# A convolution kernel whose half sums m1 and m2 move into two PSUM tiles of one bank each

## The chip, the cores and the metric

One core of one Trainium2 chip. The metric is the device time of one execution in microseconds. Medians are over four to eleven executions. A ratio is the mean time of one kernel's runs over the mean of the other's of the same rounds, so it is not quite the ratio of the medians quoted beside it.

## The reference, cut to what matters

```python
w   = (v1 + v2).reshape(OUT_CH * N, IN_CH, 3, 3)      # U quantised in two steps
act = conv_general_dilated(gn(x), w, padding=1, feature_group_count=5)
return x + act        # x: (160, 128, 32, 32) fp32, gn: group norm without affine
```

That is 160 images of 128 channels and 32 x 32 pixels, in five sets of 32 that each have their own 128 x 128 x 3 x 3 weights. Each image is normalised, convolved and added to itself.

## The kernel before

The vertical direction of the 3 x 3 filter is computed on pairs of rows. TensorE makes two half sums per image, m1 and m2 (16 x 32 fp32 for each of 128 channels, one PSUM bank each). The even rows of the output start from m1 + m2 and the odd rows from m1 - m2. TensorE then adds the rest of the convolution on top, in a two-bank PSUM tile `eo`, of which there are two. PSUM is the memory into which TensorE writes its sums; a half sum fills one bank of it. To evacuate a tile is to read it out of PSUM, so that TensorE can write it again; the residual is the addition of the convolution to x. Images come in two kinds. A "combined" image has both of its 16-bit parts combined beforehand, so m2 takes six matmuls and m1 six. A "direct" image has three and three, and a longer rest.

```python
self.pair = self.ps_m.tile([P, 2, self.H // 2, self.W], F32, tag="m", name="m")   # two banks, one tile

def sums_of_pairs(self, i):                    # TensorE: m2 first, then m1
    for a, kind in ((1, self.DIFF), (0, self.SUM)):
        for col in self.COLS: ...              # 3 or 6 matmuls into m[:, a]

def leave(self, i):                            # ScalarE: m2 to SBUF
    self.nc.scalar.copy(m2, self.pair[:, 1])

def pairs(self, i, between=lambda: None):      # VectorE: m1 from PSUM, m2 from SBUF
    m1, m2 = self.pair[:, 0], self.m2.pop(i)
    nc.vector.tensor_add(rows[:, :, 0], m1, m2)
    between()                                  # one other small instruction
    nc.vector.tensor_sub(rows[:, :, 1], m1, m2)
```

A steady iteration i, by engine, in the order of the program, in which the traces show them as well:

```
TensorE: m2(i+1), m1(i+1), rest of the convolution of i
ScalarE: statistics, sum(i-1) out of PSUM, copy of m2(i+1), high part of i+3, statistics
VectorE: low part of i+2 (direct: its combinings), add and sub for i+1, combine(i+4)
POOL:    accumulating DMA of sum(i-1) onto x in SBUF;   SyncE: store, then load ahead
```

Tracking of reads and writes goes by tile. In the built program TensorE signals once, after the last matmul of m1. ScalarE's copy of m2 waits for that signal, and the next m2 waits for VectorE's subtraction, which of this tile reads m1 only.

## Time and profile before

| | before |
|---|---|
| time, median (range) | 1043.2 us (1041.9 to 1045.2) |
| TensorE / VectorE / ScalarE busy | 953.6 / 931.0 / 897.1 us of 1038.9 |
| waits around m: VectorE / ScalarE / TensorE | 84.5 / 83.2 / 48.8 us |
| ScalarE waiting for loads of images | 11.1 us, three times |

The lines behind the busy times and the waits around m are shown in the prediction. The shares of the chain of work that ended last, of which the three engines hold 83%:

```profile
ACT junk L192 <- DMA xt<-in_x_dram: 11.1, 3, 10.2
```

```profile
PE 42%; DVE 29%; ACT 12%; issue 7%; POOL 5%; DMA 5%; SPq 0%; POOLq 0%; ACTq 0%; DVEq 0%
```

Of the page's part on DMA (packets, MB, share of the time of 16 engines), these two:

```profile
q1 hardware_dynamic: 45168, 173.09, 49.1%
q0 software_dynamic: 22032, 80.23, 39.9%
```

The first queue carries loads and stores. The second carries the accumulating transfers within SBUF, which add the convolution to x.

### The profile page before, as it was taken

The numbers are of one execution on the slowest core, as the hardware profiler recorded it, in microseconds if no ns is written. First come the engines' busy times: TensorE is split into PE (matmuls) and PEld (weight loads), VectorE is DVE, ScalarE is ACT, GpSimd is POOL, SyncE is SP. The second block draws the span as 40 slices with busy tenths as digits, with TensorE's granted clock in tenths as the row PEclk, the third lists the DMA queues.
The fourth block names the chain that finished last, engine by engine and source line by source line (L and its number), as shares of the span: only waits on it lengthen the run. The fifth ranks groups of instructions, "written<-read, shape, count | busy, mean of one in ns | idle before, by whom it ended". The sixth has DMA issues, their size and how long they took to land.

```text
span 1038.9 us, 16017 instructions
## 1 busy us (share of the span) xinstructions
PE 953.6 (92%) x5935; PEld 573.6 (55%) x5935; DVE 931.0 (90%) x1253; ACT 897.1 (86%) x1215; POOL 433.7 (42%) x599
## 2 busy tenths in 40 slices
PE   2899998999999999999999999999899999999996
PEld 1445555555555555555555555565555555565554
DVE  7999999998989999889999998899999988888884
ACT  4779898989889898998998989888998999998561
POOL 4546653452515172634443544417262623243320
PEclk9999999999999999999999999999999999999999
DMA  9439899989999989999999999998999999997664
GB/s 367 174 102 246 241 245 264 234 234 272 291 250 256 266 233 258 251 273 263 245 261 256 251 258 257 283 260 236 258 264 244 240 269 273 272 258 210 172 162 145
DMA packets 67287, 254.42 MB, mean 245 GB/s; under 512 B 5248, under 2 KB 5248, under 8 KB 67200
## 3 DMA queue, kind: packets, MB, share of 16 engines
q1 hardware_dynamic: 45168, 173.09, 49.1%
q0 software_dynamic: 22032, 80.23, 39.9%
q8 instruction: 48, 0.79, 0.3%
q14 instruction: 39, 0.32, 0.1%
HBM read 89.19 MB, written 83.89 MB: 167 GB/s over the span
## 4 chain that ended last, share of the span: by engine, by line
PE 42%; DVE 29%; ACT 12%; issue 7%; POOL 5%; DMA 5%; SPq 0%; POOLq 0%; ACTq 0%; DVEq 0%
PE m L670 18%; PE eo L634 15%; PE eo L670 7%; DVE eo L738 4%; DVE vl L587 4%; DVE eo L740 4%; ACT vh L581 4%; DVE v L570 3%; ACT junk L199 3%; DMA xt<-in_x_dram 3%; DVE v L573 2%; DVE v L576 2%; DMA xt<-sum 2%; ACT m L728 2%; DVE lo L594 2%
## 5 line engine op out<-in xcount | busy, mean ns | idle before, releaser
L670 PEld LDWEIGHTS <-wt 128*128 128x128 f16 x4428 | 428.9, 98 | 295.9 <-DVE eo L740 62.2
L767 POOL DMA_DIRECT2D xt<-sum x153 | 138.1, 903 | 434.5 <-ACT sum L754 424.6
L634 PE MATMUL eo<-hi,wt 128*128 128x496 f16 (+3 forms) x1260 | 300.9, 375 | 1.1 <-ACT wt L479 0.6
L670 PE MATMUL m<-vh,wt 128*128 128x512 f16 x534 | 203.4, 381 | 48.2 <-DVE eo L740 48.0
L587 DVE SCALAR_TENSOR_TENSOR vl<-v,rstd,vh 128x2048 f16<-128x2048 f32 x89 | 208.7, 2345 | 1.2 <-ACT vh L581 1.1
L670 PE MATMUL eo<-vl,wt 128*128 128x248 f16 (+1 forms) x1068 | 204.7, 273 | 0.0
L670 PE MATMUL eo<-vh,wt 128*128 128x248 f16 (+1 forms) x1068 | 204.6, 273 | 0.0
L670 PE MATMUL m<-vl,wt 128*128 128x512 f16 x534 | 202.9, 380 | 0.0
L634 PEld LDWEIGHTS <-wt 128*128 128x128 f16 x1332 | 130.0, 99 | 127.9 <-ACT wt L479 1.8
L738 DVE TENSOR_TENSOR eo<-m,m 128x512 f32<-128x512 f32 x157 | 109.1, 695 | 84.6 <-ACT m L728 84.5
L581 ACT ACTIVATE vh<-v,rstd 128x2048 f16<-128x2048 f32 x89 | 178.6, 2007 | 4.6 <-POOL v L560 3.7
L199 ACT ACTIVATE junk<-xt,mv 128x1024 f16<-128x1024 f32 x152 | 173.7, 1143 | 0.2
L192 ACT ACTIVATE junk<-xt 128x1024 f16<-128x1024 f32 x152 | 160.7, 1057 | 14.2 <-DMA xt<-in_x_dram 11.1
L754 ACT ACTIVATE sum<-eo 128x1024 f32<-128x1024 f32 x153 | 154.6, 1010 | 14.2 <-PE eo L670 13.3
L728 ACT COPY m<-m 128x512 f32<-128x512 f32 x157 | 91.4, 582 | 84.1 <-PE m L670 83.2
L670 PE MATMUL eo<-rows,wt 128*128 128x248 f16 (+1 forms) x816 | 122.7, 273 | 0.0
L740 DVE TENSOR_TENSOR eo<-m,m 128x512 f32<-128x512 f32 x157 | 108.6, 691 | 1.2
L570 DVE TENSOR_TENSOR v<-xt 128x960 f32<-128x960 f32 x89 | 102.2, 1149 | 0.0
L670 PE MATMUL m<-rows,wt 128*128 128x496 f16 (+1 forms) x408 | 99.4, 380 | 0.8 <-DVE eo L740 0.8
L594 DVE TENSOR_TENSOR lo<-z,hi 128x1024 f16<-128x1024 f32 x71 | 86.7, 1221 | 0.3 <-ACT hi L536 0.3
L560 POOL TENSOR_SCALAR v<-xt,ngm 128x32 f32<-128x32 f32 x89 | 81.5, 916 | 0.0
L559 POOL TENSOR_SCALAR v<-xt,ngm 128x32 f32<-128x32 f32 x89 | 76.4, 858 | 0.0
(112 smaller groups left out, 899.2 us busy)
## 6 DMA issues: line engine op xcount, KB each, us to landing
xt<-in_x_dram SPq DMA_DIRECT2D x78, 1024.0 KB, 8.9
out_dram<-xt SPq DMA_DIRECT2D x78, 1024.0 KB, 5.2
xt<-sum POOLq DMA_DIRECT2D x153, 512.0 KB, 6.5
range<-in_L_conv_U_dram SPq DMA_DIRECT2D x4, 576.0 KB, 6.7
u<-in_L_conv_U_dram SPq DMA_DIRECT2D x4, 576.0 KB, 11.6
xt<-in_x_dram SPq DMA_DIRECT2D x4, 512.0 KB, 9.5
out_dram<-xt SPq DMA_DIRECT2D x3, 512.0 KB, 2.7
u<-in_L_conv_U_dram SPq DMA_DIRECT2D x2, 288.0 KB, 3.1
```

The source lines that it names most:

```text
L192: self.nc.scalar.activation(junk, image, ACTF.Copy, scale=-1.0 / image.shape[1], accum_out=self.mv[:, j, 0:1],)
L199: self.nc.scalar.activation(junk, image, ACTF.Square, bias=self.mv[:, j, 0:1], accum_out=self.mv[:, j, 1:2],)
L570: nc.vector.tensor_sub(v[:, W:last], x[:, : last - W], x[:, 2 * W :])
L581: self.nc.scalar.mul(vh, self.v[i], st.rstd[:, j])
L587: self.nc.vector.scalar_tensor_tensor(vl, self.v[i], st.rstd[:, j], self.hi[i], ALU.mult, ALU.subtract)
L634: nc.tensor.matmul(target[:, h, r0 - h0 : r1 - h0, c0:c1], self.wts[n, col][:, k, :], tile[:, s0 : s0 + r1 - r0, c0 + dw : c1 + dw], start ...
L670: self.nc.tensor.matmul(target[:, :, c0:c1], self.wts[n, col][:, kind, :], source[:, :, c0 + dw : c1 + dw], start=start, stop=stop, skip_g ...
L728: self.nc.scalar.copy(m2, self.pair[:, 1])
L738: nc.vector.tensor_add(rows[:, :, 0], m1, m2)
L740: nc.vector.tensor_sub(rows[:, :, 1], m1, m2)
L754: nc.scalar.mul(self.sum[i], eo, 0.5)
L767: self.nc.gpsimd.dma_start(self.image(i), self.sum.pop(i), accum_op=ALU.add)
```

## The change

The intent is that ScalarE's copy of m2 waits for m2 alone, and that the next m2 waits for that copy alone. Then m2 and the evacuation of m1 no longer hold each other up. For a direct image VectorE's third combining also moves in front of the add, because the next m2 reads it. The diff, cut:

```diff
-        self.pair = self.ps_m.tile([P, 2, self.H // 2, self.W], F32, tag="m", name="m")
+        self.pair = [
+            ps_m.tile([P, self.H // 2, self.W], F32, tag=name, name=name) for name in ("m1", "m2")
+        ]
...  (m[:, a], self.pair[:, 0] and self.pair[:, 1] become self.pair[a]; one residual of the start is cut in two)
                 elif i + 2 < self.imgs:
                     self.low_part(i + 2)
                     take(later, 1)
-                    rows = self.combinations(i + 2)
-                    take(rows, 2)
+                    run(self.combinations(i + 2))
...
-                    self.pairs(i + 1, lambda: take(later if self.combined(i + 2) else rows, 1))
-                run(rows)
+                    self.pairs(i + 1, lambda: take(later, int(self.combined(i + 2))))
```

More of the change, by code (lines that the diff above doesn't have):

```diff
@@ L374, in __init__ @@
         self.ps_eo = pool("ps_eo", 2, space=PSUM)
-        self.ps_m = pool("ps_m", 1, space=PSUM)
+        ps_m = pool("ps_m", 1, space=PSUM)
         self.ps_stat = pool("ps_stat", 1, space=PSUM)
@@ L634, in taps @@
                 nc.tensor.matmul(
-                    target[:, h, r0 - h0 : r1 - h0, c0:c1],
+                    self.bank(target, h)[:, r0 - h0 : r1 - h0, c0:c1],
                     self.wts[n, col][:, k, :],
@@ L644, in bank_pair, with bank @@
         return self.ps_eo.tile([self.P, 2, self.H // 2, self.W], F32, tag="eo", name=f"eo{i}")
+    def bank(self, target, h):
+        return target[h] if target is self.pair else target[:, h]
     def warm_up(self, count):
@@ L651, in warm_up @@
             self.nc.tensor.matmul(
-                self.pair[:, 0].rearrange("p i w -> p (i w)"), zeros[:, :128],
+                self.pair[0].rearrange("p i w -> p (i w)"), zeros[:, :128],
                 zeros[:, :512], start=True, stop=True,
@@ L683, in sums_of_pairs @@
     def sums_of_pairs(self, i):
-        m = self.pair
         both = self.both(i)
@@ L690, in sums_of_pairs @@
                     self.product(
-                        m[:, a], i, kind, st[:, a], col,
+                        self.pair[a], i, kind, st[:, a], col,
                         col == self.COLS[0] and j == 0,
@@ L727, in leave @@
         m2 = self.evac.tile([self.P, self.H // 2, self.W], F32, tag="m2", name=f"m2_{i}")
-        self.nc.scalar.copy(m2, self.pair[:, 1])
+        self.nc.scalar.copy(m2, self.pair[1])
         self.m2[i] = m2
@@ L734, in pairs @@
         nc = self.nc
-        m1, m2 = self.pair[:, 0], self.m2.pop(i)
+        m1, m2 = self.pair[0], self.m2.pop(i)
         eo = self.eo[i] = self.bank_pair(i)
@@ L748, in residual @@
         nc = self.nc
-        eo = self.eo.pop(i).rearrange("p h r w -> p (h r w)")
+        eo = self.eo.pop(i)
         del self.hi[i]
@@ L753, in residual @@
             self.sum[i] = self.sums.tile([self.P, 1024], F32, tag="sum", name=f"sum{i}")
-            nc.scalar.mul(self.sum[i], eo, 0.5)
+            nc.scalar.mul(self.sum[i], eo.rearrange("p h r w -> p (h r w)"), 0.5)
             return
         xj = self.image(i)
-        halves = [slice(0, 512), slice(512, 1024)] if i == self.imgs - 1 else [slice(0, 1024)]
-        for h in halves:
+        if i == self.imgs - 1 or eo is self.pair:
+            parts = [
+                (slice(h * 512, h * 512 + 512), self.bank(eo, h).rearrange("p r w -> p (r w)"))
+                for h in range(2)
+            ]
+        else:
+            parts = [(slice(0, 1024), eo.rearrange("p h r w -> p (h r w)"))]
+        for h, part in parts:
             nc.vector.scalar_tensor_tensor(
-                xj[:, h], eo[:, h], 0.5, xj[:, h], ALU.mult, ALU.add
+                xj[:, h], part, 0.5, xj[:, h], ALU.mult, ALU.add
             )
@@ L965, in run @@
             else:
-                rows = iter(())
                 if self.combined(i + 2):
```

## The prediction

> **What bounds the kernel now.** I read the page first (busy shares, slices), then the list of waits, then busy times over seven stretches in the steady middle, then one timeline of two iterations, then the DMA queues and their landing times.
>
> ```profile
> PE 953.6 (92%) x5935; PEld 573.6 (55%) x5935; DVE 931.0 (90%) x1253; ACT 897.1 (86%) x1215; POOL 433.7 (42%) x599
> DMA  9439899989999989999999999998999999997664
> ```
>
> No engine is full and four are nearly so. The kernel treats one image per iteration, so the question is which wait keeps three engines at about nine tenths. The list of waits answers it:
>
> ```profile
> DVE eo L738 <- ACT m L728: 84.5, 83, 2.1
> ACT m L728 <- PE m L670: 83.2, 82, 7.1
> PEld L670 <- DVE eo L740: 62.2, 49, 3.0
> PE m L670 <- DVE eo L740: 48.8, 38, 2.8
> ```
>
> These four rows (total us, times, longest) are one ring around the tile m, which holds both half sums: TensorE writes m2 and m1 (L670), ScalarE copies m2 out (L728), VectorE writes m1+m2 and m1-m2 into eo (L738, L740), and only then TensorE writes m again. Nearly everything else in that list is POOL waiting, which is off the path, or start-up. The load-weights row is the same stall as the matmul row and is not added to it.
>
> In seven stretches of one seven-image pattern each (435.55 to 739 us: four "combined" images, three "direct" ones) the sum over 303.45 us is
>
> ```profile
> sum 303.45, PE 286.96 PEld 174.12 DVE 276.51 ACT 278.96 POOL 126.31; mean PE 40.99 PEld 24.87 DVE 39.50 ACT 39.85 POOL 18.05
> ```
>
> so a pattern takes 43.35 us (303.45/7), of which TensorE works 41.0, ScalarE 39.9, VectorE 39.5. The ring costs 2.4 us per pattern on TensorE, 5 to 6%. The timeline shows two iterations of it (start, length, engine, line, and in brackets the idle time before):
>
> ```profile
> 519.74 0.38 PE L670 MATMUL m<-vh,wt 128*128 128x512 f16 x1
> ...
> 521.04 0.38 PE L670 MATMUL m<-vh,wt 128*128 128x512 f16 x1
> ...
> 522.34 0.38 PE L670 MATMUL eo<-vh,wt 128*128 128x256 f16 x2
> 522.54 0.58 ACT L728 COPY m<-m 128x512 f32<-128x512 f32 x1 [1.30 <-PE m L670]
> ...
> 528.14 0.58 ACT L728 COPY m<-m 128x512 f32<-128x512 f32 x1
> ...
> 528.75 0.70 DVE L738 TENSOR_TENSOR eo<-m,m 128x512 f32<-128x512 f32 x1 [1.34 <-ACT m L728]
> ...
> 529.91 0.69 DVE L740 TENSOR_TENSOR eo<-m,m 128x512 f32<-128x512 f32 x1
> ...
> 530.65 0.39 PE L670 MATMUL m<-vh,wt 128*128 128x512 f16 x1 [1.60 <-DVE eo L740]
> ```
>
> The six matmuls of m2 run from 519.74 to 521.04 and the six of m1 to 522.34. The copy reads m2 alone, yet it starts at 522.54, after m1. At 530.65 TensorE begins the next m2, which ScalarE had copied out by 528.72; it waited 1.60 us for VectorE, which was reading m1. Both waits are for the other half of the tile.
>
> **What the Trainium skill says.** "PSUM — Partial Sum Buffer", section "PSUM bank collisions raise a hardware error": two engines must not touch one bank at once, while different banks run clean; its rule is to guard by bank. Each half of m is 512 fp32, one bank, so the hardware allows what the change does. The trace agrees as far as it goes: at 524.15 VectorE writes one eo pair while TensorE writes the other, with no loss on either. "Perfetto Trace Analysis", section "Matmuls", says that independent matmul groups should rotate through different banks so that evacuating one overlaps the next; before the change the evacuation overlaps nothing of the next m. The same page, "Identifying the Most-Contended Engine", warns that matmul busy time is a poor measure of headroom. So I took the floor from start to start: 0.215 us for a 496 to 512 column matmul (519.74, 519.96, 520.18), 0.109 for a 248 to 256 column one. "TensorE: Matmul & The Clock Gate", section "Back-to-back issue gap", gives about 131 ns sustained for 512 columns and 216 ns isolated; this trace shows the second, and I use the measured 0.215.
>
> **The change part by part.** No matmul, copy or add is added or taken away in the steady loop. One residual of the start (direct image 2) is cut into two halves, about 1.4 us in place of 1.2, once.
>
> (a) TensorE's m2 group no longer waits for VectorE. In the built program before the change, its first weight load waits for VectorE's subtraction; after it, the group waits for ScalarE's copy and for the new image's low part, and only m1's first matmul waits for the subtraction. A m2 group is 6 x 0.215 = 1.29 us for a combined image, 3 x 0.215 = 0.65 for a direct one. For each recorded TensorE stall on L740 after 60 us I take the smaller of the stall and that length: 40 stalls, 49.0 us together, give 42.0 us (almost all stand before a combined image; most are 1.0 to 1.7 us). This is the direct gain if nothing takes its place.
>
> (b) ScalarE's copy is released by the last m2 matmul, not the last m1: 1.29 or 0.65 us earlier. The 83.2 us wait has a start-up piece (7.1) and otherwise means about 0.9 us, so most of it goes. The copy leads to the add, so VectorE's 84.5 us shrink too. It is not added to (a), because it lies on the same ring; it is what keeps (a) from being eaten at m1. Working 519.74 to 530.65 again by hand: copy at 521.24 (ScalarE finishes its previous sum then) in place of 522.54; the next copy, without idle time in between, 1.3 earlier at 526.84; add at 527.45, subtraction done by 529.3; TensorE, free about 529.05, starts m2 there and m1 at 530.35. The whole 1.60 us stall is gone and every engine is 1.3 to 1.6 us ahead.
>
> (c) The direct image's third combining (L611, about 0.41 us) moves from between add and subtraction to in front of the add. Same work, same engine. It fills idle time where VectorE waits for the copy, and with (a) it is needed: the next m2 of a direct image reads it. Worth 0 to 0.4 us per direct image, mostly hidden; I count 0.
>
> (d) Added: one more semaphore update and wait per image. Both sit on instructions that exist; 0.
>
> Sum before losses: about 42 us.
>
> **The rivals.**
> 1. The engines meet their own floors. Per pattern ScalarE's work plus its small gaps is about 40.5 us, TensorE's 41.0, so a pattern cannot fall much below 41.2, 2.1 us less than now; with 21 patterns between 60 and 950 us that is 45 us, above the 42, but three engines at 97 to 100% with one buffer each never fit perfectly. The stretch 850 to 950 us shows TensorE at 97.64 of 100 us with this ring still there. At that density a pattern takes 41.0/0.976 = 42.0: a gain of 1.35 x 21 = 28 us, plus about 4 in the tail, where three stalls of 1.72 us stand: 32 us. I hold this the likeliest limit.
> 2. DMA. Slices read 9 of 10 and the middle moves about 259 GB/s at a share near 0.95; at 42 us a pattern that becomes about 267 and 0.98. One stretch (651 to 694 us) already ran at 276 GB/s and 1.02 with no stall of its own, and the skill page above calls the busy share misleading. But latency counts: a load of two images takes
>
> ```profile
> xt<-in_x_dram SPq DMA_DIRECT2D x78, 1024.0 KB, 8.9
> SPq L772 <- DMA xt<-sum: 848.8, 94, 13.7
> ```
>
> and it is issued behind a store that waits for the accumulation. From the sum of an image to the first reading of the load behind it there are four iterations. In the trace, the 32 loads issued from 450 to 850 us landed a median 3.4 us before ScalarE first read them, six of them under 1 us. An iteration 0.2 us shorter takes 0.8 us of that, so perhaps a quarter of the loads come just too late, by some tenths: 2 to 8 us lost. If the queues also slow down, the loss could reach 20 and the result falls to within 2%.
> 3. The wait moves to m1. If VectorE or ScalarE is the late one throughout, m1 waits for the subtraction as m2 did before, and (a) gains nothing. The hand working of (b) speaks against it; for it speaks that half of the copies start with no idle time before them, ScalarE itself being late. It would make about 1030.
> 4. Waits for POOL (the variances) stay, about 6 us.
>
> **Range and chances.** 1043.8 minus 42 would be 1002; density and DMA take 8 to 15 of it, giving a gain of about 31 and **1013 us**. Range 998 to 1029: the low end has the ring gone and little in its place, the high end has rival 2 or 3 taking half. Faster by over 2% means under 1022.9, a gain of 21 us, half of (a): 0.78. Within 2%: 0.21. Slower: 0.01, since no work and no wait is added.
>
> **What would show it.** Right: TensorE's wait on the subtraction falls from 48.8 to under 15 us and stands before m1; ScalarE's wait on the m2 group falls from 83 to under 40; TensorE is at 94 to 96% of the span; the seven-image pattern takes about 42 us. Wrong: a new row of ScalarE waiting on the loads above 15 us (rival 2), or m1 waiting as long as m2 did (rival 3). (c) is wrong if VectorE's idle time before the add grows for direct images.

## More of the kernel before

The kernel before was run again with each set of experiments, on whichever chip they fell, and its median lay between 1042.6 and 1048.2 us. Compare kernels of different sets by their ratios.

## The result, and the profile after

1005.9 us (1002.2 to 1008.8), ratio 0.9639 with a 95% interval from 0.9603 to 0.9675: 3.6% faster. The 1013 forecast was 7 us too high, inside its range. A second set of the same kernel gave 1007.0 us and 0.9649. Line numbers have moved: L670 is now L675 (matmuls of m and eo), L728 is L732 (the copy), L738 and L740 are L742 and L744 (add and subtraction).

Busy times on the page after:

```profile
PE 954.3 (95%) x5935; PEld 577.8 (57%) x5935; DVE 935.8 (93%) x1254; ACT 888.2 (88%) x1215; POOL 448.1 (44%) x599
```

The work is the same as before to within 1% on each of the three engines, so the gain is idle time. The list of waits after (engine and line that waits, whom it waits for, total us, times, longest):

```profile
ACT junk L192 <- DMA xt<-in_x_dram: 38.7, 19, 11.5
DVE eo L742 <- ACT m L732: 34.2, 29, 3.3
...
ACT sum L758 <- PE eo L675: 21.4, 18, 3.8
...
ACT m L732 <- PE m L675: 15.4, 17, 7.1
...
PE m L675 <- DVE eo L744: 8.8, 22, 0.6
...
PE m L675 <- DVE vl L589: 5.9, 8, 1.5
```

Beside the four rows of the prediction: TensorE's wait for the subtraction fell from 48.8 to 8.8 us, ScalarE's wait for the m group from 83.2 to 15.4, and VectorE's wait for the copy from 84.5 to 34.2. In place of them one row has grown most: ScalarE, at the first reading of an image, waits 38.7 us for its load, against 11.1. Both figures contain one start-up piece of about 11 us, so the new part is about 27 us. (ScalarE's wait for TensorE's finished eo, the third row shown, went from 13.3 to 21.4.)

The chain that ended last tells the same. DMA, 5% of it before, is now its largest part:

```profile
DMA 24%; DVE 20%; ACT 18%; PE 14%; POOL 13%; issue 11%; SPq 1%; POOLq 0%; ACTq 0%; DVEq 0%
```

Where the remaining wait stands is seen in the timeline after, around a combined image:

```profile
539.96 0.58 ACT L732 COPY m<-m 128x512 f32<-128x512 f32 x1
...
540.59 0.38 PE L675 MATMUL m<-vh,wt 128*128 128x512 f16 x1 [0.69 <-ACT m L732]
...
541.43 0.69 DVE L742 TENSOR_TENSOR eo<-m,m 128x512 f32<-128x512 f32 x1
541.57 0.38 PE L675 MATMUL m<-vl,wt 128*128 128x512 f16 x1 [0.61 <-DVE vl L589]
...
542.56 0.69 DVE L744 TENSOR_TENSOR eo<-m,m 128x512 f32<-128x512 f32 x1
...
543.31 0.38 PE L675 MATMUL m<-vh,wt 128*128 128x512 f16 x1 [0.49 <-DVE eo L744]
```

The first matmul of m2 (540.59) starts when the copy ends at 540.54. The subtraction ends only at 543.25. The wait for it is now at 543.31, on m1's first matmul, and lasts 0.49 us, because m2's matmuls run while VectorE works. The two new waits in front (for the copy and for the image's low part `vl`) are real dependencies. The stretch is not a typical one: ScalarE had waited 2.16 us for a load at 532.40. Over the whole span TensorE waits 8.8 us for the subtraction, 5.9 for `vl` and 3.3 for the copy.

Seven stretches of one seven-image pattern each, cut from copy to copy between 440.92 and 736.91 us:

```profile
sum 295.99, PE 286.55 PEld 174.40 DVE 278.78 ACT 276.32 POOL 134.84; mean PE 40.94 PEld 24.91 DVE 39.83 ACT 39.47 POOL 19.26
```

A pattern takes 42.28 us (295.99/7) against 43.35, with 40.94 us of TensorE's work in it. (The prediction's stretches were not cut at copies; seven patterns cut from copy to copy took 43.24 each before.) The DMA share, which as the profile counts it can come out a little over 1, is 0.97 to 1.02 in five of these stretches, of which I show two (length, then busy us and instructions per engine; last granted clock, DMA share, GB/s):

```profile
568.15:610.62 42.47, 41.20 (x261) 25.16 (x260) 41.95 (x55) 39.56 (x56) 21.21 (x25) 1.00 1.00 273
610.62:654.43 43.81, 43.39 (x282) 27.38 (x281) 37.53 (x46) 39.16 (x55) 18.01 (x26) 1.00 1.02 271
```

### The profile page after: what moved, and what is told of

It is laid out like the page before. It is cut to its first block, busy times and chain, and to the rows that moved or that the text cites. A ratio compares the mean times of both kernels' runs of the same rounds, so it can differ in the third digit from the quotient of the medians.

```text
span 1007.1 us, 16173 instructions
## 1 busy us (share of the span) xinstructions
PE 954.3 (95%) x5935; PEld 577.8 (57%) x5935; DVE 935.8 (93%) x1254; ACT 888.2 (88%) x1215; POOL 448.1 (44%) x599
## 2 busy tenths in 40 slices
DMA packets 67288, 254.43 MB, mean 253 GB/s; under 512 B 5248, under 2 KB 5248, under 8 KB 67200
## 3 DMA queue, kind: packets, MB, share of 16 engines
q1 hardware_dynamic: 45168, 173.09, 50.3%
q0 software_dynamic: 22032, 80.23, 41.1%
## 4 chain that ended last, share of the span: by engine, by line
DMA 24%; DVE 20%; ACT 18%; PE 14%; POOL 13%; issue 11%; SPq 1%; POOLq 0%; ACTq 0%; DVEq 0%
DMA xt<-in_x_dram 13%; DMA xt<-sum 10%; ACT vh L583 5%; PE m L675 4%; PE eo L636 4%; PE eo L675 4%; ACT junk L199 4%; ACT sum L758 4%; DVE v L572 3%; DVE eo L742 2%; DVE eo L744 2%; POOL rstd L235 2%; ACT m L732 2%; DVE vl L589 2%; DVE v L575 2%
## 5 line engine op out<-in xcount | busy, mean ns | idle before, releaser
L675 PEld LDWEIGHTS <-wt 128*128 128x128 f16 x4428 | 432.9, 98 | 262.2 <-issue 33.2
L675 PE MATMUL m<-vh,wt 128*128 128x512 f16 x534 | 202.5, 379 | 11.1 <-DVE eo L744 7.4
L675 PE MATMUL m<-vl,wt 128*128 128x512 f16 x534 | 202.6, 379 | 6.0 <-DVE vl L589 5.9
L675 PE MATMUL eo<-vl,wt 128*128 128x248 f16 (+1 forms) x1068 | 204.6, 273 | 0.0
L675 PE MATMUL eo<-vh,wt 128*128 128x248 f16 (+1 forms) x1068 | 204.5, 273 | 0.0
L192 ACT ACTIVATE junk<-xt 128x1024 f16<-128x1024 f32 x152 | 160.7, 1057 | 41.5 <-DMA xt<-in_x_dram 38.7
L758 ACT ACTIVATE sum<-eo 128x1024 f32<-128x1024 f32 x153 | 154.4, 1009 | 21.8 <-PE eo L675 21.4
L742 DVE TENSOR_TENSOR eo<-m,m 128x512 f32<-128x512 f32 x157 | 108.7, 693 | 42.1 <-ACT m L732 34.2
L675 PE MATMUL eo<-rows,wt 128*128 128x248 f16 (+1 forms) x816 | 122.7, 273 | 0.0
L744 DVE TENSOR_TENSOR eo<-m,m 128x512 f32<-128x512 f32 x157 | 109.3, 696 | 3.4
L732 ACT COPY m<-m 128x512 f32<-128x512 f32 x157 | 90.8, 578 | 15.6 <-PE m L675 15.4
L675 PE MATMUL m<-rows,wt 128*128 128x496 f16 (+1 forms) x408 | 100.6, 380 | 1.5 <-DVE eo L744 1.3
L561 POOL TENSOR_SCALAR v<-xt,ngm 128x32 f32<-128x32 f32 x89 | 83.6, 939 | 0.0
L538 ACT CAST hi<-z 128x1024 f16<-128x1024 f32 x71 | 74.4, 1047 | 1.7
```

Of the source, the lines that this page charges most:

```text
L192: self.nc.scalar.activation(junk, image, ACTF.Copy, scale=-1.0 / image.shape[1], accum_out=self.mv[:, j, 0:1],)
L675: self.nc.tensor.matmul(target[:, :, c0:c1], self.wts[n, col][:, kind, :], source[:, :, c0 + dw : c1 + dw], start=start, stop=stop, skip_g ...
L732: self.nc.scalar.copy(m2, self.pair[1])
L758: nc.scalar.mul(self.sum[i], eo.rearrange("p h r w -> p (h r w)"), 0.5)
```

## The experiments

### Set 1: which part of the change, and the new wait

**Two tiles, VectorE's order as before** (the second and third hunk of the diff undone).

> The two tiles alone; VectorE's order is that of the kernel before (a direct image's third combining stands between the add and the subtraction). Theory: the split carries the gain, because nearly all stalls stood before combined images, whose m2 group needs no combining: 1003 to 1012 us, within 5 us of the full change. Rival (the order carries a large part, since m2 of a direct image waits for its combinings): 1015 to 1030 us, with TensorE waiting for the combining before m2 of direct images.

Measured: 1012.9 us, ratio 0.969 (0.9643 to 0.9737). That is 1 us above the range written. The split carries most of the gain. The sign written for the rival is there, but small: TensorE waits for the third combining.

```profile
PE m L675 <- DVE rows L613: 3.9, 5, 1.6
```

Whether the order adds a few us was left open here, and the last set takes it up.

**The order alone** (one tile m; the second and third hunk applied).

> The order alone; one tile m of two banks as before. Theory: no gain, since both waits for the other half stay: 1038 to 1046 us, TensorE still waits 45 to 50 us for the subtraction. Rival (order helps by itself, because the combining now fills VectorE's idle time before the add): 1030 to 1036 us.

Measured: 1047.6 us, ratio 1.0029 (1.0010 to 1.0049). There is no gain; it is 0.3% slower, and 2 us above the range written. TensorE's wait for the subtraction stayed, and was even a little over the 45 to 50 us written:

```profile
ACT m L728 <- PE m L670: 81.5, 78, 7.1
...
PE m L670 <- DVE eo L740: 56.0, 44, 2.8
```

**Matmuls of m2 and m1 alternating** (two tiles, new order).

```diff
-        for a, kind in ((1, self.DIFF), (0, self.SUM)):
-            for col in self.COLS:
-                for j, (_, st) in enumerate(both):
+        for col in self.COLS:
+            for j, (_, st) in enumerate(both):
+                for a, kind in ((1, self.DIFF), (0, self.SUM)):
```

> Two tiles and the new order, but the matmuls of m2 and m1 alternate, so that m2 ends one matmul before m1 and m1's first matmul follows m2's first at once. Same work, right result. Theory (the gain is the length of the m2 group by which TensorE and ScalarE no longer wait): nearly all of it is lost, 1030 to 1044 us. Rival (the gain is in smaller or fewer waits by tile, whatever the order of the matmuls): 1003 to 1012 us.

Measured: 1037.3 us, ratio 0.9916 (0.9891 to 0.9941). More than three quarters of the gain is lost, although the tiles are split as in the change. So two tiles alone are not enough. What pays is that m2 as a whole stands in front of m1.

**Loads two images earlier** (`LOAD_LEAD = 20` in place of 18).

> The changed kernel with loads issued two images earlier (one store earlier in the DMA queue of SyncE), same eleven buffers. In the changed kernel's trace ScalarE waits 38.7 us for loads, against 11.1 before, and the loads issued from 430 to 820 us land a median 1.2 us before their first reading. Theory (the loop is now bound by the latency from accumulation through store to load): the loads land several us earlier, ScalarE's wait for them falls to about 12 us and the time to 985 to 998 us. Rival (the wait for the loads only takes the place of idle time that ScalarE would have anyway, or the DMA queues are full): 1001 to 1009 us.

Measured: 1018.5 us, ratio 0.9726 (0.9693 to 0.9759), slower than the changed kernel. The expected time was missed by 20 us. The trace says why (the last line is of SyncE's queue, loads waiting for the store of their buffer):

```profile
DVE nn L99 <- DMA u<-in_L_conv_U_dram: 24.8, 2, 12.9
...
ACT junk L192 <- DMA xt<-in_x_dram: 20.9, 11, 11.6
```

```profile
SPq L412 <- DMA out_dram<-xt: 588.8, 69, 13.3
```

ScalarE's wait for images did fall. But SyncE's queue works in order, and the load of an image now stood there waiting for its buffer's store, with the next set's weights queued behind it. VectorE waited 12.9 and 11.9 us for weights. The granted clock was lower too just after these stalls, 0.77 from 450 to 470 us and 0.60 from 660 to 665, and 0.989 over the span against 0.998 in the changed kernel, so part of the loss may be clock. Before the first of these stalls the trace holds the best evidence. From the 29th to the 57th copy, four patterns, this kernel took 162.86 us, or 40.7 per pattern. The changed kernel, which was at the same point to within half a microsecond, took 167.94 us, or 42.0. Those two stretches, the changed kernel first:

```profile
231.91:399.85 167.94, 166.06 (x1054) 102.41 (x1053) 160.51 (x211) 156.67 (x216) 68.04 (x92) 1.00 0.99 269
```

```profile
231.47:394.33 162.86, 162.21 (x1028) 99.90 (x1027) 159.68 (x211) 157.41 (x215) 68.22 (x92) 1.00 0.99 266
```

TensorE is busy 162.21 of 162.86 us in the second, so at that point it is full. The DMA engines moved about the same in both, 269 and 266 GB/s at a share of 0.99. A pattern needs 11.13 MB (254.43 MB / 160 x 7), which at 40.7 us is 273 GB/s. The difference came out of the lead of the loads. They landed 10.5 to 14.5 us before their first reading at the start of this stretch (loads 22 to 24), about 3 us before it near the end (loads 36 and 37), and 0.1 us at loads 39 and 40; the stall for weights then rebuilt the lead. In the changed kernel the loads from 430 to 820 us landed a median 1.2 us ahead.

### Set 2: parts (a) and (b) of the prediction, each without the other

Both edits only reorder the same matmuls on top of the changed kernel. m2 and m1 stand here for the lists of their matmuls.

```diff
 # "a alone": the last matmul of m2 behind m1, so the copy is released as late as before
-        m2 + m1
+        m2[:-1] + m1 + m2[-1:]
 # "b alone": the first matmul of m1 in front, so TensorE waits for the subtraction before both
-        m2 + m1
+        m1[:1] + m2 + m1[1:]
```

The changed kernel again, on the same chip:

> The changed kernel again, as the measure of the other three on the same chip. Every theory: 1002 to 1009 us (ratio 0.960 to 0.968).

Measured: 1007.0 us, ratio 0.9649 (0.9633 to 0.9665).

> The changed kernel with the last matmul of m2 put behind m1: m2's other matmuls still start without waiting for VectorE's subtraction (part a), but ScalarE's copy is released only at the end of m1, as before (part b undone). Same matmuls, right result. Theory of the prediction (a is the direct gain; b only keeps it from being eaten): 1012 to 1028 us, ScalarE waiting 50 to 85 us for the m groups again. Rival 1 (only a counts): 1003 to 1010. Rival 2 (the early release of the copy is what counts): 1030 to 1042.

Measured: 1030.6 us, ratio 0.9876 (0.9856 to 0.9896). The gain is 1.24% out of 3.51.

> The changed kernel with the first matmul of m1 put before m2: TensorE waits for the subtraction before nearly all of both groups, as before (part a undone), but the copy is released five matmuls (for a direct image two) before the end of the groups (part b kept nearly whole). Theory of the prediction: 1015 to 1030 us, TensorE waiting 20 to 35 us for the subtraction, since the earlier copy brings the subtraction forward. Rival 1 (only a counts): 1035 to 1044. Rival 2 (only b counts): 1003 to 1012.

Measured: 1025.8 us, ratio 0.9844 (0.9827 to 0.9861). The gain is 1.56%. The waits of "a alone" and then of "b alone" (the copy is L735 there, the subtraction L747):

```profile
ACT m L735 <- PE m L675: 52.6, 44, 7.1
...
PE m L675 <- DVE eo L747: 21.5, 44, 0.8
```

```profile
PE m L675 <- DVE eo L747: 34.8, 40, 2.8
...
ACT m L735 <- PE m L675: 29.1, 32, 7.1
```

Each alone takes away a part of the other's wait too, as the prediction had it for one ring. Neither carries the change: 1.24 and 1.56 sum to 2.80%, and together they give 3.51. Part of the missing 0.71 may come from the edits: of a combined image's six matmuls each keeps five for its part, of a direct image's three it keeps two. So each run refutes one rival: "a alone" shows that a is not all that counts, "b alone" that b is not. By its time, "a alone" lies 2.6 us beyond the range that I had written for the theory, at the lower edge of the second rival's; it is "b alone", 14 us from that rival's range, that excludes it. These sizes hold under the transfer limit shown below. Even "a alone" has ScalarE waiting 33.5 us for loads, so part of what it freed may have been lost there.

**Loads earlier, and the weights earlier too** (two images before a set begins).

```diff
-            if n + 1 < N_SETS:
-                if b == (2 if n == 0 else 0):
-                    self.load_set(n + 1)
+            if n == 0 and b == 2:
+                self.load_set(1)
+            if b == self.per_set - 2 and n + 2 < N_SETS:
+                self.load_set(n + 2)
+            if n + 1 < N_SETS:
```

> The changed kernel with loads two images earlier, and with the weight loads of sets 2 to 4 issued two images before the set begins, so that they no longer stand behind a load that waits for its buffer. In the run with earlier loads alone, VectorE waited 24.8 us for two such weight loads, while ScalarE's wait for images fell from 38.7 to 20.9 us. Theory (the loop is bound by image loads, and the loss of that run was the weight loads): the wait for weights goes, 988 to 999 us. Rival (ScalarE's wait for loads is idle time that it would have anyway): 1002 to 1009 us.

Measured: 1019.0 us, ratio 0.9756 (0.9708 to 0.9805). A miss again. The stalls for weights went, but ScalarE's waits for images came back, 51.4 us in 29 waits:

```profile
ACT junk L192 <- DMA xt<-in_x_dram: 51.4, 29, 11.6
DVE eo L742 <- ACT m L732: 45.7, 34, 5.6
```

The lead was gone by the 35th load here too, and the 12 us stall for weights that had rebuilt it in the run before no longer came. So in these two runs issuing loads earlier in one in-order queue did not help. It spent the lead at the start and then blocked stores, in the first run weights too. Why this run is also about 1% slower than the changed kernel was not tested.

### Set 3: are the transfers the new bound?

**Accumulating transfers cut to half their columns**, in the changed kernel and in the kernel before. Their outputs are wrong, which doesn't matter for the times. No engine's work changes.

```diff
-            self.nc.gpsimd.dma_start(self.image(i), self.sum.pop(i), accum_op=ALU.add)
+            self.nc.gpsimd.dma_start(
+                self.image(i)[:, :512], self.sum.pop(i)[:, :512], accum_op=ALU.add
+            )
```

> The changed kernel with each accumulating transfer cut to half its columns; the result is wrong on purpose, the transfers move 214 in place of 254 MB, and no engine's work changes. In the run with loads two images earlier the lead of the loads over their first reading, 10 to 20 us, melted to 0.1 us within ten to fifteen loads, while a seven-image pattern took 40.4 to 41 us as long as it lasted; in the changed kernel it takes about 42. Theory (the changed kernel is bound by what the DMA engines can move): ScalarE's wait for loads falls to 12 to 20 us, the pattern to 40.4 to 41, the time to 975 to 992 us. Rival (the 42 us are the three engines' own misfit, and waiting for loads only takes the place of other idle time): 1000 to 1008 us.

Measured: 994.0 us, ratio 0.9483 (0.9452 to 0.9514). This lies 2 us above the written range, in a set whose kernel before took 1048.2 us (the record gives the chip of set 2, where it took 1042.6); by the ratio it is 989 us at the first set's 1043.2. The waits:

```profile
DVE eo L742 <- ACT m L732: 20.1, 22, 1.3
...
ACT m L732 <- PE m L675: 17.0, 24, 7.1
ACT junk L192 <- DMA xt<-in_x_dram: 11.9, 2, 11.7
```

Only the start-up wait for loads is left. The same four patterns as in the run with earlier loads took 162.84 us here (from 231.85 to 394.69), the same as there to 0.02 us. This time the pace holds to the end. Seven patterns from 435.28 us on:

```profile
sum 288.70, PE 285.56 PEld 175.04 DVE 278.72 ACT 277.41 POOL 140.49; mean PE 40.79 PEld 25.01 DVE 39.82 ACT 39.63 POOL 20.07
```

41.24 us a pattern with TensorE working 40.79 of them. TensorE is now the bound, at 99%.

> The same cut in the kernel before (wrong on purpose). Theory (before the change the ring around the tile m set the pace, and the transfers were hidden): 1036 to 1044 us, within 1% of the kernel before. Rival (the transfers held the kernel before as well): 1010 to 1030 us.

Measured: 1048.5 us, ratio 1.0008 (0.9975 to 1.0041). The same cut is worth nothing in the kernel before, where TensorE's wait for the subtraction stood at 48.5 us with the cut. The transfers became a bound only when the ring was opened.

**One residual in seven taken from the transfers**: VectorE adds it from PSUM. The result is right.

```diff
-        return i < self.FIRST or i >= self.imgs - LAST
+        return (
+            i < self.FIRST or i >= self.imgs - LAST
+            or (2 * self.STEADY <= i < self.THIRDS and i % 7 == 0)
+        )
```

> The changed kernel, right result, with one residual of each seven (images 14 to 145 divisible by 7, 19 in all) added by VectorE straight from PSUM, as the last four images do it: minus 1.0 us of ScalarE and minus one 512 KB transfer per pattern, plus 1.2 us of VectorE, in the iteration where VectorE has least to do. Theory (bound by transfers, 4.5% fewer bytes in those patterns): 990 to 1001 us. Rival (VectorE, with 39.5 us of a pattern's 42, takes their place): 1005 to 1015 us.

Measured: 1009.1 us, ratio 0.9631 (0.9599 to 0.9664), the same as the change. ScalarE's wait for loads fell to 20.8 us, but VectorE's busy time rose from 935.8 to 957.6 us. Other waits grew in place of those for loads (in the changed kernel these three are 21.4, 5.5 and 8.8 us):

```profile
ACT sum L761 <- PE eo L675: 31.3, 32, 3.6
...
ACT vh L583 <- DVE v L578: 15.3, 19, 2.3
PE m L675 <- DVE eo L744: 13.9, 27, 1.4
```

The time lies in the rival's range, so VectorE took the gain as far as this run tells. No experiment with a right result beats the change by more than the noise.

**Two tiles with the old order, more rounds.**

> The two tiles alone with VectorE's old order, as in the first such run, with more rounds to settle what the order is worth: the full change stands at ratios 0.964 and 0.965, the first run of this at 0.969 with an interval from 0.964 to 0.974. Theory (the order is worth a few us, because m2 of a direct image no longer waits for a combining behind the add): 0.967 to 0.972. Rival (nothing): 0.963 to 0.966.

Measured: 1015.6 us, ratio 0.9682 (0.9655 to 0.9710), against 0.9639 and 0.9649 of the full change in other sets. Both runs of the split alone lie above both runs of the full change, by about 0.4%, or 4 us. The intervals overlap, so I take the order to be worth a few us, not a settled figure. In the traces, the split alone has TensorE waiting 3.9 and 3.6 us for the third combining, a row that both traces of the full change lack, and 10.0 and 9.7 us for POOL's variances, against 4.2 and 3.9. Which of the two makes the 4 us was not tested.

## Why the prediction was right

The mechanism and the direction were right; that the number came so near is in part luck, since two terms were off in opposite directions.

**What bounds the kernel before.** Right. The ring around m set the pace. The order alone and the lighter transfers left it at 1.003 and 1.001. Opening the ring gave 3.6%.

**(a) TensorE's m2 no longer waits, 42 us.** The 42 us were near the idle time that the ring holds. With the transfers made lighter, TensorE's idle time, from the program's first instruction to its last matmul, falls from 78.2 us (before) to 35.7 us (the run with half accumulations), 42.5 less; in the changed kernel it is 45.7. These three sums are taken from the traces as the time in which no matmul runs. They come short of the time won: against the kernel before with the same half accumulations the span falls by 52.6 us (1044.6 to 992.0), of which 44.8 are idle time and 7.8 are busy time (957.1 to 949.3). A likely reason is how a stall is counted: a matmul's record lasts 0.38 us, but in a stream the next starts after 0.215, so each stall hides up to 0.17 us under "busy". Counted in the trace from start to start, the 48.8 us of stalls before m are about 55. But I gave the 42 us to (a) and called (b) only "what keeps (a) from being eaten". That was the wrong division, and the step of (a) that failed: alone, (a) gives 1.24% and (b) 1.56%, and it takes both to give 3.51%.

**(b) The earlier copy.** Right in direction and in the waits: ScalarE's wait for m fell to 15.4 us (I wrote under 40), and TensorE's to 8.8 (I wrote under 15), standing before m1 as I wrote.

**(c) The order, counted 0.** Probably a few us too low: about 4 us, just visible in the two runs without it. My criterion was that VectorE's idle time before the add must not grow for direct images. Counted from the traces for these alone it is 32.8 us before, 25.9 and 25.4 with the split alone, and 21.7 and 22.8 with the order as well, so it holds.

**(d) The added semaphore update and wait, 0.** Nothing in the traces shows a cost. No run measured it apart.

**Rival 1, the engines' own floors.** A term that was mis-sized. The floor itself, 41.2 us a pattern, was close; the discount from it was not. I took the density of one stretch before (97.6%) as the limit, 42.0 us a pattern and a gain of 32 us. With lighter transfers the engines fit at 41.24 us a pattern (40.7 in the four patterns with earlier loads), 99% of TensorE, and the kernel gains 5.2%, or 54 us by the ratio.

**Rival 2, the transfers, 2 to 8 us.** Also mis-sized, the other way, and the sign that I had written for "wrong" came: a row of ScalarE waiting on the loads above 15 us. I expected a quarter of the loads to come late by some tenths. ScalarE waits about 27 us more for loads, in waits of up to 3.9 us after start-up. In time the transfers take about 1.6%, from 0.964 to 0.948, some 16 to 17 us. So the limit that I named second was the one that holds at 42 us. The two errors had opposite signs, and the sum, 31 us against 37, came out better than its terms: that is luck.

**Rivals 3 and 4.** The wait did move to m1 but shrank to 0.6 us at most. TensorE's wait for POOL (the variances) was 8.1 us over the whole span and is 4.2.

What stays open: the experiments show that the transfers hold the changed kernel, but not fully whether by their rate or by the latency of the chain from sum to accumulation to store to load, since the cut of the accumulations shortens both (a load lands in a median 8.0 us there, 9.4 in the changed kernel). A lead of 10 to 14 us melting at 266 GB/s moved against 273 needed speaks for the rate; the 588.8 us in which SyncE's loads stood behind their buffers' stores in that run show that the chain through the eleven buffers is tight as well.

## What to carry to other kernels

If the halves of a buffer are written and read in turn by different engines, give each half its own tile, and put in front the half that is freed first. Here tracking by tile had made the copy wait for both halves' matmuls and the next m2 for the last reader of the other half. Size such a change by the idle time of the ring as a whole, not by one of its links. Before promising the sum, look at how far the loads land ahead of their use: here a median lead of 3.4 us with the DMA engines at a share near 0.95 became the next bound. Moving fewer bytes helped here (with a wrong result), and an earlier place in the same in-order queue did not.

## What the Trainium skill lacked or had wrong

- "Perfetto Trace Analysis", "Identifying the Most-Contended Engine", advises HBM utilization in place of occupancy for DMA. The page counts it as all DMA throughput over 358 GB/s; after the change that is 253 of 358, 71%, and HBM itself carried 172, since 80 of the 254 MB are accumulations within SBUF. Yet the transfers cost about 1.6%. The share of the 16 engines (0.97 to 1.02 in five of seven patterns) pointed to it, but does not settle it either: before the change it was 0.91 to 1.02 in seven patterns, and halving the accumulations gained nothing there (ratio 1.0008).
- "DMA: Bandwidth & Descriptors", "SDMA does more than copy", lists addition among the operations but no rate for it within SBUF. In the kernel before, accumulating transfers took 39.9% of the engines' time for 80.23 MB, and loads and stores 49.1% for 173.09 MB: 1.75 times the time per byte.
- "TensorE: Matmul & The Clock Gate", "Back-to-back issue gap", gives about 131 ns per matmul of 512 columns in a stream with weight loads; here the median from start to start is 0.216 us for 512 columns, before and after, which is what the section gives for an isolated matmul.
